# A two-layer codebook convolution: the copies of the extra numerators, the two range watches and an image's last step are rearranged

## The chip, the core and the metric

The kernel runs on one core of a Trainium2 chip. The metric is the device time of one execution in microseconds; three executions of the kernel before give a median of 4144.86 us (4143.25 to 4152.45). Engines are named as in the profile: PE multiplies matrices, PEld loads its weights, DVE is the vector engine, ACT the scalar engine, POOL is GpSimd, SP only issues transfers here. Each engine works through its own queue in order.

## What is computed

Input x has 16 images of 256 channels on 28 x 28 pixels. Each image is normalized in groups of 8 channels, goes through two layers that approximate a 3 x 3 convolution, through a squeeze-and-excitation gate, and is added to x. One layer replaces each channel's 9-pixel patch by a softmax mixture of 16 centroids, and looks the mixture up in a table:

```python
def amm_conv3x3(x, centroids, w_sub):
    patches = conv_general_dilated_patches(x, (3, 3), (1, 1), 'SAME')
    p = patches.reshape(B, C, 9, Ho * Wo).transpose(0, 3, 1, 2)
    d = sum(p * p)[..., None] - 2.0 * einsum('bncs,cks->bnck', p, centroids) + sum(centroids * centroids)
    attn = softmax(-d, axis=-1)
    lut = einsum('cks,cso->cko', centroids, w_sub)
    return einsum('bnck,cko->bno', attn, lut)

out = relu(bn1(amm_conv3x3(_gn(x), centroids1, wsub1)))
out = bn2(amm_conv3x3(out, centroids2, wsub2))
out = relu(se_layer(out) + _gn(x))
x = x + out
```

The last two lines are an image's last step: gate times layer output, plus the normalized image, relu, plus the image.

## The kernel before, in words

The 256 channels lie in 11 groups (`ORDER`: groups 9 and 10 first, then 0 to 8), the 784 pixels in two runs of 384 and 400 columns (`PXT`). One layer of one image is a stage of 2 x 11 = 22 **slots**, a slot being one group of one run. Stages follow in the order layer 0 of image 0, layer 0 of image 1, layer 1 of image 0, layer 0 of image 2, layer 1 of image 1 and so on.

The group of a slot s passes these steps, each on its engine:

- `patches`: POOL issues a transfer of the group pair's patches from DRAM, four slots ahead (nine in layer 1).
- Layer 1 only, five slots ahead: `a_logits` (PE), `a_turn` (DVE, two transpositions, L397), `a_max` (DVE, two reductions, L405), then once per pair `m_turn`, `m_out`, `m_in`, which bring the largest logit back into the patches. This is the extra pass for the maxima. Layer 0 has none; there two watches guard the range instead.
- `b_logits` (PE, L378), `b_exp` (ACT, two exponentials, L444): slot s, positions 5 and 6.
- `b_num` (PE, L454): numerators and sums, slot s + 1, position 3. It needs the exponentials.
- `b_turn` (DVE), slot s + 1, position 4: one transposition out of PSUM into a tile `t` (L466), the reciprocal `rc` of three columns of sums per block (L470), and in layer 0 the two watches, L473 on the sums in `t` and L474 on `rc`, which put their maxima into a column of `ext`.
- `c_scale`, slot s + 1, position 4: for groups 9 and 10 POOL writes scaled numerators into `qx` (L501); these are the extra numerators. For groups 0 to 8 POOL scales `t` in place (L487), and ACT copies five extra numerators per half from `qx` over the columns of sums in `t` (L490).
- `c_turn` (DVE, L511), slot s + 2, position 2, before the next group's L466: transposes `t` back. It needs POOL's scaling and ACT's copy.
- `c_look` (PE, L522): the lookups, 36 per run, five slots later, three or four of them in a slot; the last ones of a run are followed by `evacuate` on ACT (L535, L545).

The order on every engine's queue is written out by hand: a `Plan` collects jobs under (slot, position) and `emit` issues them sorted by this key, and within one key in the order in which they were put there. So in slot s + 1 ACT's queue holds the copy L490 of group s, then the exponentials of group s + 1 behind it. `prep` places four shifts (ACT, positions 4 and 6) and 15 patch writes (ACT's transfer queue, position 8) in a stage. PSUM pairs rotate in a ring of three: two take the logits of a group, one its numerators.

`norm` does an image's group statistics. `close` finishes an image after layer 1, in slots of the next stage (layer 0 of the image after the next): `se_hidden` and `se_gate` in two slots at position 9, then in two slots `finish(b, k)`, for one half of the channels each: L351 on ACT over 784 columns, L352 and L353 on DVE over 784, and then `store` (POOL, L356).

After the plan a test of `ext` on DVE and PE decides whether a slow, always guarded version of the whole computation runs; with these inputs it does not.

Of the kernel before, what the change touches and what calls it, by code (L numbers as in the profile page):

```python
# [9 lines left out]
AF = mybir.ActivationFunctionType  # L10
ALU = mybir.AluOpType
AX = mybir.AxisListType
# [5 lines left out]
HW = H * W  # L18
# [7 lines left out]
NBG = 9  # L26
# [4 lines left out]
S_LIM = 1e26  # L31
# [8 lines left out]
SUM = 27  # L40
# [23 lines left out]
def kernel(  # L64
# [28 lines left out]
    nc = tc.nc  # L93
    B, C, _ = x.shape
# [22 lines left out]
    def bank():  # L117
        return pair()[:, 0]
# [10 lines left out]
    xs = {}  # L129
# [70 lines left out]
    ext = const.tile([P, 2, NSTAT], F32, name="ext")  # L200
# [106 lines left out]
    ys = {}  # L307
# [34 lines left out]
        nc.vector.tensor_scalar_mul(nb, nb, -1.0)  # L342
        se[b] = gt, nb

    def finish(b, k):

        gt, nb = se[b]
        y, _ = ys[b]
        _, rstd = nrm[b]
        xt = xs[b]  # L350
        nc.scalar.activation(y[:, k], y[:, k], AF.Identity, bias=nb[:, k : k + 1], scale=gt[:, k : k + 1])  # L351
        nc.vector.scalar_tensor_tensor(y[:, k], xt[:, k], rstd[:, k : k + 1], y[:, k], op0=ALU.mult, op1=ALU.add)  # L352
        nc.vector.scalar_tensor_tensor(y[:, k], y[:, k], 0.0, xt[:, k], op0=ALU.max, op1=ALU.add)  # L353

    def store(b, ob):
        nc.gpsimd.dma_start(ob.rearrange("(b p) n -> p b n", p=P), ys.pop(b)[0])  # L356
# [29 lines left out]
    def blocks(u):  # L386
        return (u["px"][1] + 31) // 32
# [74 lines left out]
    def b_turn(u, gi):  # L462

        nb = blocks(u)
        t = npool.tile([P, 26, 32], F32, tag="nt", name="nt")
        nc.vector.transpose(  # L466
            t[:, : 2 * nb].rearrange("p (h b) r -> p h (b r)", h=2), u.pop(("nm", gi))[:, :, : 32 * nb]
        )
        rc = small.tile([P, 26, 3], F32, name="rc")
        nc.vector.reciprocal(rc[:, : 2 * nb], t[:, : 2 * nb, SUM : SUM + 3])  # L470
        if u["col"][gi] is not None:
            col = u["col"][gi]
            nc.vector.tensor_reduce(ext[:, 0, col : col + 1], t[:, : 2 * nb, SUM : SUM + 3], axis=AX.XY, op=ALU.max)  # L473
            nc.vector.tensor_reduce(ext[:, 1, col : col + 1], rc[:, : 2 * nb], axis=AX.XY, op=ALU.max)  # L474
        u["nt", gi] = t, rc

    qxs = {}

    def c_scale(u, gi):
        g, nb = u["groups"][gi], blocks(u)  # L480
        t, rc = u["nt", gi]
        key = u["key"]
        if g == NBG:
            qxs[key] = xqpool.tile([P, 13, EXTRA], F32, tag="qx", name="qx")
        if g < NBG:
            v = t[:, : 2 * nb, :SUM].rearrange("p b (j s) -> p b j s", s=9)
            nc.gpsimd.tensor_tensor(v, v, rc[:, : 2 * nb].unsqueeze(3).to_broadcast([P, 2 * nb, 3, 9]), ALU.mult)  # L487

            w = qxs[key][:, :nb, 10 * g : 10 * g + 5]
            nc.scalar.copy(  # L490
                t[:, : 2 * nb].rearrange("p (h b) r -> p h b r", h=2)[:, :, :, SUM:],
                bass.AP(w.tensor, w.offset, [list(w.ap[0]), [5, 2], list(w.ap[1]), list(w.ap[2])]),
            )
            if g == NBG - 1:
                qxs.pop(key)
        else:
            u.pop(("nt", gi))
            for h in range(2):
                e = 2 * (g - NBG) + h
                nj = 3 if e < 3 else 1  # L500
                nc.gpsimd.tensor_tensor(  # L501
                    qxs[key][:, :nb, 27 * e : 27 * e + 9 * nj].rearrange("p b (j s) -> p b j s", s=9),
                    t[:, h * nb : (h + 1) * nb, : 9 * nj].rearrange("p b (j s) -> p b j s", s=9),
                    rc[:, h * nb : (h + 1) * nb, :nj].unsqueeze(3).to_broadcast([P, nb, nj, 9]), ALU.mult,
                )

    def c_turn(u, gi):
        nb = blocks(u)
        t, _ = u.pop(("nt", gi))
        q = qpool.tile([P, 832], F32, tag="q", name="q")  # L510
        nc.vector.transpose(q[:, : 64 * nb], t[:, : 2 * nb].rearrange("p b r -> p (b r)"))  # L511
        u["q", gi] = q
# [44 lines left out]
    class Plan:  # L557
# [4 lines left out]
        def at(self, slot, pos, f, *a):  # L562
            self.jobs.setdefault((slot, pos), []).append((f, a))
# [6 lines left out]
        def stage(self, l, b, pat, s0, maxed, cols):  # L570
            at = self.at
            for pi, px in enumerate(PXT):
                n0 = s0 + pi * NG
                of = {}
                for ui, gs in enumerate(UNITS):
                    u = {
                        "l": l, "b": b, "pi": pi, "px": px, "pat": pat, "key": (l, b, pi),
                        "groups": gs, "n": self.units, "col": [cols.pop() if cols else None for _ in gs],
                    }
                    self.units += 1  # L580
                    n = n0 + 2 * ui
                    for gi, g in enumerate(gs):
                        s = n + gi
                        of[g] = u, gi
                        if maxed:
                            at(s - LB, 0, a_logits, u, gi)
                            at(s - LB, 1, a_turn, u, gi)
                            at(s - LB, 8, a_max, u, gi)
                        at(s, 5, b_logits, u, gi)
                        at(s, 6, b_exp, u, gi)  # L590
                        at(s + 1, 3, b_num, u, gi)
                        at(s + 1, 4, b_turn, u, gi)
                        at(s + 1, 4, c_scale, u, gi)
                        if g < NBG:
                            at(s + 2, 2, c_turn, u, gi)
                    at(n - LEAD - (LB if maxed else 0), 9, patches, u)
                    if maxed:
                        e = n + len(gs) - 1 - LB
                        at(e, 9, m_turn, u)
                        at(e, 9, m_out, u)  # L600
                        at(e + 1, 5, m_in, u)
                for k, (g, o, h) in enumerate(LOOKS):
                    s, r = divmod(k * NG, len(LOOKS))
                    early = maxed and 2 * r < len(LOOKS)
                    at(n0 + LC + s, 1 if early else 7, c_look, *of[g], o, h)
# [12 lines left out]
        def close(self, b, ob, te):  # L618
            self.at(te + 1, 9, se_hidden, b)
            self.at(te + 2, 9, se_gate, b)  # L620
            for k in range(NB):
                self.at(te + 3 + k, 9, finish, b, k)
            self.at(te + 5, 9, store, b, ob)

    stages = [(0, 0)]
    for b in range(B):
# [21 lines left out]
    for si, (l, b) in enumerate(stages):  # L648
        t = si * NS
# [14 lines left out]


    worst = small.tile([P, 2], F32, name="worst")
    nc.vector.tensor_reduce(worst, ext, axis=AX.X, op=ALU.max)
    good = small.tile([P, 2], F32, name="good")
    nc.vector.tensor_scalar(good, worst, S_LIM, None, op0=ALU.is_le)
    ps = bank()  # L670
    nc.tensor.matmul(ps[0:1, 0:2], lhsT=ones, rhs=good, start=True, stop=True)
    count = small.tile([1, 1], F32, name="count")
# [83 lines left out]
```

## Time and profile before

| what | value |
|---|---|
| median of three executions | 4144.86 us (4143.25 to 4152.45) |
| the profiled execution, its time | 4143.49 us |
| its span from first to last instruction | 4141.9 us |
| instructions | 81729 |
| busy: PE, DVE, ACT, POOL | 3777.2, 3244.5, 1424.4, 1283.7 us |
| mean granted clock of PE | 0.975 of full speed |
| chain that ended last | PE 44%, DVE 38%, issue 6%, ACT 5%, DMA 4% |
| DMA over the span | 148 GB/s |

Busy is the time in which an engine executes; a matmul's end is modelled. The chain is followed back from the last instruction, at each step to what released it. A timeline row reads: start in us, length in us, engine, line of the kernel, operation, output<-input, shapes, how many instructions are merged in it, and in brackets how long the engine had stood idle before it and what ended this. Windows give each engine's busy time in a stretch, then the mean granted clock of PE, the share of DMA engines' time and the rate.

### The profile page before, as it was taken

How to read it: one execution, taken by the hardware profiler on the slowest of the kernel's cores; microseconds unless marked ns; L12 is line 12 of the kernel's file. 1: busy time of each engine (PE TensorE's matmuls, PEld its weight loads, DVE VectorE, ACT ScalarE, POOL GpSimd, SP SyncE). 2: the span in 40 equal slices, each digit the busy share in tenths (PEclk: the TensorE clock that was granted, in tenths of full speed). 3: DMA queues.
4: the chain of work that ended last, by engine and by line, in shares of the span. 5: the costliest groups of instructions: out<-in, count | busy, mean ns of one | idle time of the engine just before them, and what ended most of it. 6: DMA issues, size and time to landing. Idle time of an engine off the chain costs nothing.

```text
span 4141.9 us, 81729 instructions
## 1 busy us (share of the span) xinstructions
PE 3777.2 (91%) x33042; PEld 1342.1 (32%) x33042; DVE 3244.5 (78%) x4644; ACT 1424.4 (34%) x2385; POOL 1283.7 (31%) x1314
## 2 busy tenths in 40 slices
PE   2989999999998999999999999999999999999897
PEld 0333333333333333333333333333333333333232
DVE  2669697795978969688795977969779696887897
ACT  1433433334343333433334333342433334333232
POOL 2332323323233232333323233232332323333222
PEclk7999999999999999999999999999999999999999
DMA  7454545445453455434555454454534554345431
GB/s 245 150 165 145 163 117 155 159 133 183 130 166 121 136 183 147 154 114 142 178 150 170 116 156 151 132 183 129 166 121 137 182 153 155 107 140 179 147 89 55
DMA packets 361805, 611.05 MB, mean 148 GB/s; under 512 B 205370, under 2 KB 217802, under 8 KB 361162
## 3 DMA queue, kind: packets, MB, share of 16 engines
q0 software_dynamic: 75520, 321.15, 24.4%
q10 hardware_dynamic: 80490, 236.05, 17.2%
q1 hardware_dynamic: 205408, 48.52, 5.7%
q8 instruction: 263, 4.31, 0.4%
q14 instruction: 124, 1.02, 0.1%
HBM read 338.50 MB, written 271.94 MB: 147 GB/s over the span
## 4 chain that ended last, share of the span: by engine, by line
PE 44%; DVE 38%; issue 6%; ACT 5%; DMA 4%; ACTq 2%; POOL 0%; DVEq 0%; SPq 0%; POOLq 0%
PE acc L522 20%; PE pair L378 12%; PE pair L454 11%; DVE z L397 9%; DVE nt L466 8%; DVE mx L405 8%; DVE q L511 4%; DVE rc L470 4%; ACT e L444 4%; ACTq L301 2%; DMA pat<-side 2%; DVE mt L414 1%; DMA pt<-dm 1%; DVE y L352 1%; ACT y L351 1%
## 5 line engine op out<-in xcount | busy, mean ns | idle before, releaser
L522 PE MATMUL acc<-q,ws 128*128 128x384 f32 (+1 forms) x4608 | 1787.3, 520 | 6.0 <-ACT im L535 6.0
L378 PE MATMUL pair<-pt,wd 31*64 31x400 f32 (+1 forms) x16896 | 1335.2, 521 | 186.0 <-ACT e L444 77.6
L487 POOL TENSOR_TENSOR nt<-nt,rc 128x648 f32<-128x648 f32 (+1 forms) x576 | 773.5, 1343 | 1874.4 <-DVE ext L473 957.2
L444 ACT ACTIVATE e<-pair 128x768 f32<-128x768 f32 (+1 forms) x1408 | 1084.3, 818 | 401.7 <-PE pair L378 390.9
L522 PEld LDWEIGHTS acc<-q,ws 128*128 128x128 f32 x4608 | 813.6, 192 | 975.4 <-issue 566.4
L490 ACT COPY nt<-qx 128x120 f32<-128x120 f32 (+1 forms) x576 | 183.8, 319 | 2216.0 <-DVE rc L470 1145.5
L466 DVE STREAM_TRANSPOSE nt<-pair 128x768 f32<-128x768 f32 (+1 forms) x704 | 701.2, 996 | 283.1 <-PE pair L454 279.5
L454 PE MATMUL pair<-e,cw 64*32 64x384 f32 (+1 forms) x11264 | 791.3, 507 | 131.7 <-ACT e L444 127.9
L511 DVE STREAM_TRANSPOSE q<-nt 128x768 f32<-128x768 f32 (+1 forms) x576 | 569.6, 989 | 331.1 <-POOL nt L487 319.8
L397 DVE STREAM_TRANSPOSE z<-pair 128x768 f32<-128x768 f32 (+1 forms) x704 | 668.8, 985 | 70.4 <-PE pair L378 67.0
L378 PEld LDWEIGHTS pair<-pt,wd 31*64 31x64 f32 x16896 | 335.0, 131 | 1102.3 <-DVE z L397 385.5
L405 DVE TENSOR_REDUCE mx<-z 128x48 f32<-128x768 f32 (+1 forms) x704 | 644.1, 957 | 0.0
L470 DVE RECIPROCAL rc<-nt 128x72 f32<-128x72 f32 (+1 forms) x704 | 438.5, 623 | 24.2
L365 POOL DMA_DIRECT2D pt<-pat x384 | 299.4, 780 | 472.5 <-PE pair L378 405.5
L454 PEld LDWEIGHTS pair<-e,cw 64*32 64x32 f32 x11264 | 161.6, 105 | 646.3 <-ACT e L444 461.2
L501 POOL TENSOR_TENSOR qx<-nt,rc 128x324 f32<-128x324 f32 (+3 forms) x256 | 166.2, 668 | 466.5 <-DVE rc L470 339.3
L352 DVE SCALAR_TENSOR_TENSOR y<-xt,gn_rstd,y 128x784 f32<-128x784 f32 x32 | 33.1, 1034 | 86.1 <-ACT y L351 86.1
L414 DVE STREAM_TRANSPOSE mt<-mx 128x256 f32<-128x256 f32 x192 | 81.2, 423 | 6.5
L474 DVE TENSOR_REDUCE ext<-rc 128x1 f32<-128x72 f32 (+1 forms) x352 | 81.4, 231 | 0.0
L289 ACT COPY side<-im 128x756 f32<-128x756 f32 x64 | 52.6, 823 | 35.3 <-DMA pat<-im 35.3
L473 DVE TENSOR_REDUCE ext<-nt 128x1 f32<-128x72 f32 (+1 forms) x352 | 60.7, 173 | 0.0
L291 ACT COPY side<-im 128x756 f32<-128x756 f32 x64 | 52.7, 825 | 7.2 <-DMA pat<-side 7.2
(63 smaller groups left out, 397.1 us busy)
## 6 DMA issues: line engine op xcount, KB each, us to landing
pt<-pat POOLq DMA_DIRECT2D x160, 800.0 KB, 5.4
pt<-pat POOLq DMA_DIRECT2D x160, 768.0 KB, 4.9
pat<-side ACTq DMA_DIRECT2D x128, 771.8 KB
pat<-im ACTq DMA_DIRECT2D x64, 771.8 KB
pat<-side ACTq DMA_DIRECT2D x64, 404.2 KB
xt<-in_x POOLq DMA_DIRECT2D x32, 784.0 KB, 7.4
pat<-side ACTq DMA_DIRECT2D x64, 367.5 KB
dm<-mt SPq DMA_DIRECT2D x320, 64.0 KB
```

Source lines behind the costliest of these rows:

```text
L365: nc.gpsimd.dma_start(pt[:, : 2 * len(gs), :n], view(u["pat"], 2 * gs[0] * P * HW + px, [[HW, P], [P * HW, 2 * len(gs)], [1, n]]),)
L378: nc.tensor.matmul(ps[i // 2][64 * h : 64 * h + 64, i % 2, :n], lhsT=wd[l][32 * i : 32 * i + rows, 2 * g + h, :], rhs=u["pt"][32 * i : 32 ...
L397: nc.vector.transpose(z[:, : 64 * nb].rearrange("p (i m) -> p i m", i=2), ps[:, :, : 32 * nb])
L405: nc.vector.tensor_reduce(u["mx"][:, a : a + 2].rearrange("p i (c b) -> p i b c", c=2)[:, :, :nb], z[:, : 64 * nb].rearrange("p (i b c k) ...
L444: nc.scalar.activation(e[:, :, :n], ps[:, :, :n], AF.Exp, scale=2.0)
L454: nc.tensor.matmul(ps[32 * i : 32 * i + 32, h, :n], lhsT=cw[l][64 * h : 64 * h + 64, g, i, :], rhs=es[i // 2][64 * h : 64 * h + 64, i % 2, ...
L466: nc.vector.transpose(t[:, : 2 * nb].rearrange("p (h b) r -> p h (b r)", h=2), u.pop(("nm", gi))[:, :, : 32 * nb])
L470: nc.vector.reciprocal(rc[:, : 2 * nb], t[:, : 2 * nb, SUM : SUM + 3])
L487: nc.gpsimd.tensor_tensor(v, v, rc[:, : 2 * nb].unsqueeze(3).to_broadcast([P, 2 * nb, 3, 9]), ALU.mult)
L490: nc.scalar.copy(t[:, : 2 * nb].rearrange("p (h b) r -> p h b r", h=2)[:, :, :, SUM:], bass.AP(w.tensor, w.offset, [list(w.ap[0]), [5, 2], ...
L511: nc.vector.transpose(q[:, : 64 * nb], t[:, : 2 * nb].rearrange("p b r -> p (b r)"))
L522: nc.tensor.matmul(accs[key][:, :n], lhsT=ws[l][:, 2 * g + h, o * P : (o + 1) * P], rhs=u["q", gi][:, 32 * nb * h : 32 * nb * h + n], star ...
```

## The change

Four things. The copy L490 leaves `c_scale` and becomes a function `c_fill` of its own, placed at position 7 of the same slot, behind the exponentials of the next group (position 6). Both watches reduce `rc`, one with maximum, one with minimum, so that `t` has one reader fewer before it is overwritten. `finish` works on half the columns, and is placed four times, in four slots; `store` follows two slots later. The closing test treats the two rows of `ext` one after the other.

```diff
--- before.py
+++ after.py
@@ -342,15 +342,15 @@
         nc.vector.tensor_scalar_mul(nb, nb, -1.0)
         se[b] = gt, nb
 
-    def finish(b, k):
+    def finish(b, k, i):
 
         gt, nb = se[b]
-        y, _ = ys[b]
+        v = slice(i * (HW // 2), (i + 1) * (HW // 2))
+        y, xt = ys[b][0][:, k, v], xs[b][:, k, v]
         _, rstd = nrm[b]
-        xt = xs[b]
-        nc.scalar.activation(y[:, k], y[:, k], AF.Identity, bias=nb[:, k : k + 1], scale=gt[:, k : k + 1])
-        nc.vector.scalar_tensor_tensor(y[:, k], xt[:, k], rstd[:, k : k + 1], y[:, k], op0=ALU.mult, op1=ALU.add)
-        nc.vector.scalar_tensor_tensor(y[:, k], y[:, k], 0.0, xt[:, k], op0=ALU.max, op1=ALU.add)
+        nc.scalar.activation(y, y, AF.Identity, bias=nb[:, k : k + 1], scale=gt[:, k : k + 1])
+        nc.vector.scalar_tensor_tensor(y, xt, rstd[:, k : k + 1], y, op0=ALU.mult, op1=ALU.add)
+        nc.vector.scalar_tensor_tensor(y, y, 0.0, xt, op0=ALU.max, op1=ALU.add)
 
     def store(b, ob):
         nc.gpsimd.dma_start(ob.rearrange("(b p) n -> p b n", p=P), ys.pop(b)[0])
@@ -470,8 +470,8 @@
         nc.vector.reciprocal(rc[:, : 2 * nb], t[:, : 2 * nb, SUM : SUM + 3])
         if u["col"][gi] is not None:
             col = u["col"][gi]
-            nc.vector.tensor_reduce(ext[:, 0, col : col + 1], t[:, : 2 * nb, SUM : SUM + 3], axis=AX.XY, op=ALU.max)
-            nc.vector.tensor_reduce(ext[:, 1, col : col + 1], rc[:, : 2 * nb], axis=AX.XY, op=ALU.max)
+            nc.vector.tensor_reduce(ext[:, 0, col : col + 1], rc[:, : 2 * nb], axis=AX.XY, op=ALU.max)
+            nc.vector.tensor_reduce(ext[:, 1, col : col + 1], rc[:, : 2 * nb], axis=AX.XY, op=ALU.min)
         u["nt", gi] = t, rc
 
     qxs = {}
@@ -485,14 +485,6 @@
         if g < NBG:
             v = t[:, : 2 * nb, :SUM].rearrange("p b (j s) -> p b j s", s=9)
             nc.gpsimd.tensor_tensor(v, v, rc[:, : 2 * nb].unsqueeze(3).to_broadcast([P, 2 * nb, 3, 9]), ALU.mult)
-
-            w = qxs[key][:, :nb, 10 * g : 10 * g + 5]
-            nc.scalar.copy(
-                t[:, : 2 * nb].rearrange("p (h b) r -> p h b r", h=2)[:, :, :, SUM:],
-                bass.AP(w.tensor, w.offset, [list(w.ap[0]), [5, 2], list(w.ap[1]), list(w.ap[2])]),
-            )
-            if g == NBG - 1:
-                qxs.pop(key)
         else:
             u.pop(("nt", gi))
             for h in range(2):
@@ -503,6 +495,17 @@
                     t[:, h * nb : (h + 1) * nb, : 9 * nj].rearrange("p b (j s) -> p b j s", s=9),
                     rc[:, h * nb : (h + 1) * nb, :nj].unsqueeze(3).to_broadcast([P, nb, nj, 9]), ALU.mult,
                 )
+
+    def c_fill(u, gi):
+
+        g, nb, key = u["groups"][gi], blocks(u), u["key"]
+        w = qxs[key][:, :nb, 10 * g : 10 * g + 5]
+        nc.scalar.copy(
+            u["nt", gi][0][:, : 2 * nb].rearrange("p (h b) r -> p h b r", h=2)[:, :, :, SUM:],
+            bass.AP(w.tensor, w.offset, [list(w.ap[0]), [5, 2], list(w.ap[1]), list(w.ap[2])]),
+        )
+        if g == NBG - 1:
+            qxs.pop(key)
 
     def c_turn(u, gi):
         nb = blocks(u)
@@ -592,6 +595,7 @@
                         at(s + 1, 4, b_turn, u, gi)
                         at(s + 1, 4, c_scale, u, gi)
                         if g < NBG:
+                            at(s + 1, 7, c_fill, u, gi)
                             at(s + 2, 2, c_turn, u, gi)
                     at(n - LEAD - (LB if maxed else 0), 9, patches, u)
                     if maxed:
@@ -619,8 +623,9 @@
             self.at(te + 1, 9, se_hidden, b)
             self.at(te + 2, 9, se_gate, b)
             for k in range(NB):
-                self.at(te + 3 + k, 9, finish, b, k)
-            self.at(te + 5, 9, store, b, ob)
+                for i in range(2):
+                    self.at(te + 3 + 2 * k + i, 9, finish, b, k, i)
+            self.at(te + 7, 9, store, b, ob)
 
     stages = [(0, 0)]
     for b in range(B):
@@ -664,9 +669,10 @@
 
 
     worst = small.tile([P, 2], F32, name="worst")
-    nc.vector.tensor_reduce(worst, ext, axis=AX.X, op=ALU.max)
     good = small.tile([P, 2], F32, name="good")
-    nc.vector.tensor_scalar(good, worst, S_LIM, None, op0=ALU.is_le)
+    for i, (op, test, lim) in enumerate(((ALU.max, ALU.is_le, S_LIM), (ALU.min, ALU.is_ge, 1.0 / S_LIM))):
+        nc.vector.tensor_reduce(worst[:, i : i + 1], ext[:, i], axis=AX.X, op=op)
+        nc.vector.tensor_scalar(good[:, i : i + 1], worst[:, i : i + 1], lim, None, op0=test)
     ps = bank()
     nc.tensor.matmul(ps[0:1, 0:2], lhsT=ones, rhs=good, start=True, stop=True)
     count = small.tile([1, 1], F32, name="count")
```

## Rows read from the trace of the kernel before

**Rows 1.** The page's first part: busy time, share of the span, instructions of each engine.
```profile
PE 3777.2 (91%) x33042; PEld 1342.1 (32%) x33042; DVE 3244.5 (78%) x4644; ACT 1424.4 (34%) x2385; POOL 1283.7 (31%) x1314
```

**Rows 2.** Windows of one image, cut at starts of L466: six slots, 2, 4, 1, 4, 4, 7, 16.
```profile
core 0: us, PE busy (x) PEld busy (x) DVE busy (x) ACT busy (x) POOL busy (x), PEclk, DMA share, GB/s
2179.89:2207.34 27.45, 27.45 (x240) 10.13 (x232) 16.32 (x20) 11.33 (x19) 10.54 (x9) 1.00 0.22 63
1958.19:1966.60 8.41, 8.41 (x86) 3.36 (x91) 3.70 (x9) 5.17 (x7) 3.25 (x5) 1.00 0.55 166
1966.60:1984.61 18.01, 16.78 (x166) 6.25 (x166) 11.31 (x21) 8.33 (x17) 7.29 (x7) 1.00 0.89 292
1984.61:1989.89 5.28, 5.28 (x59) 2.24 (x46) 3.21 (x9) 2.02 (x5) 2.03 (x2) 1.00 0.92 349
1989.89:2014.26 24.37, 20.17 (x146) 7.26 (x154) 14.87 (x26) 8.89 (x14) 7.34 (x7) 0.86 0.57 197
2014.26:2031.96 17.70, 17.48 (x162) 6.52 (x167) 9.93 (x19) 7.69 (x12) 8.36 (x10) 1.00 0.41 137
2031.96:2078.50 46.54, 44.84 (x398) 14.95 (x395) 43.45 (x65) 13.21 (x23) 13.47 (x13) 1.00 0.39 117
2078.50:2179.89 101.39, 93.94 (x860) 32.47 (x864) 98.76 (x128) 32.10 (x54) 27.32 (x29) 1.00 0.49 143
```

**Rows 3.** Waits of DVE from 1958 to 2207: us in total, times, longest.
```profile
DVE q L511 <- POOL nt L487: 19.6, 14, 1.6
DVE nt L466 <- PE pair L454: 13.5, 17, 2.6
DVE y L352 <- ACT y L351: 6.0, 2, 3.4
DVE z L397 <- PE pair L378: 3.5, 3, 2.6
```

**Rows 4.** Timeline of a light slot with a copy, 2022 to 2028.
```profile
2022.59 1.05 DVE L466 STREAM_TRANSPOSE nt<-pair 128x832 f32<-128x832 f32 x1 [1.83 <-PE pair L454]
2023.68 0.64 DVE L470 RECIPROCAL rc<-nt 128x78 f32<-128x78 f32 x1
...
2024.49 1.39 POOL L487 TENSOR_TENSOR nt<-nt,rc 128x702 f32<-128x702 f32 x1 [1.30 <-DVE ext L473]
2024.50 0.32 ACT L490 COPY nt<-qx 128x130 f32<-128x130 f32 x1 [3.32 <-DVE ext L473]
2024.72 1.56 ACT L444 ACTIVATE e<-pair 128x800 f32<-128x800 f32 x2
...
2025.60 1.61 PE L454 MATMUL pair<-e,cw 64*32 64x400 f32 x16
...
2027.28 1.05 DVE L466 STREAM_TRANSPOSE nt<-pair 128x832 f32<-128x832 f32 x1 [0.32 <-PE pair L454]
```

**Rows 5.** Timeline of two slots without a copy, 2014 to 2023.
```profile
2015.14 1.57 ACT L444 ACTIVATE e<-pair 128x800 f32<-128x800 f32 x2 [1.89 <-PE pair L378]
...
2017.75 0.90 PE L454 MATMUL pair<-e,cw 64*32 64x400 f32 x16
...
2021.58 0.91 PE L454 MATMUL pair<-e,cw 64*32 64x400 f32 x16
```

**Rows 6.** Timeline of the first of an image's two last steps, 1994 to 1997.
```profile
1994.04 1.04 ACT L351 ACTIVATE y<-y,se_nb,se_gt 128x784 f32<-128x784 f32 x1 [0.67 <-ACT e L444]
...
1995.11 1.03 DVE L352 SCALAR_TENSOR_TENSOR y<-xt,gn_rstd,y 128x784 f32<-128x784 f32 x1 [3.38 <-ACT y L351]
1996.18 0.97 DVE L353 SCALAR_TENSOR_TENSOR y<-y,xt 128x784 f32<-128x784 f32 x1
```

**Rows 7.** Groups of instructions, whole span: busy us, mean ns, idle before.
```profile
L252 DVE BATCH_NORM_STATS2 gn_st<-xt 128x6 f32<-128x392 f32 x64 | 32.1, 544 | 10.7 <-DMA xt<-in_x 10.7
```

**Rows 8.** Timeline of a heavy slot with watches, 2046 to 2049.
```profile
2046.52 0.64 DVE L470 RECIPROCAL rc<-nt 128x78 f32<-128x78 f32 x1
2047.07 0.18 DVE L473 TENSOR_REDUCE ext<-nt 128x1 f32<-128x78 f32 x1
...
2047.34 1.80 DVE L405 TENSOR_REDUCE mx<-z 128x48 f32<-128x768 f32 x2
```

## The prediction, made before the changed kernel ran

> **What bounds the kernel now.** I read the page first: PE and DVE are both busy most of the span, 91% and 78% [rows 1], so the question is which of them waits for which, and where. I then cut one image out of the trace, from 1958.19 to 2207.34 us, at the starts of the transposition L466, of which there is one per slot; 44 slots make an image, 14 whole images lie between 317 and 3840 us, and the pieces in the first two stages and the last one add about one more. The windows [rows 2] show two regimes. In 23 **heavy** slots (46.54 and 101.39 us, 6.4 us each), those with the extra pass for the maxima (L397, L405), DVE is busy 93% and 97%: DVE sets them. In the other 21, **light**, slots (27.45 + 8.41 + 18.01 + 5.28 + 24.37 + 17.70 = 101.2 us) DVE is busy 59% (59.3 us), and PE, the other candidate, is not full either: 16.78 of 18.01 in one stretch, 20.17 of 24.37 in the one with the image's last step. So a light slot is a loop of waits. DVE's waits in this image [rows 3] say with whom: 19.6 us for POOL's scaling, 13.5 us for PE's numerators (L454), 6.0 us for ACT in the last step (L351).
>
> The timeline of a light slot [rows 4] shows the loop: L466 at 2022.59, reciprocal 23.68, the copy L490 at 24.50, only then the exponentials at 24.72, numerators at 25.60 (their second half waits for the second exponential), next L466 at 27.28: 4.69 us, 0.32 of it DVE waiting for PE. The exponentials stand behind the copy in ACT's queue, and the copy needs this slot's reciprocal and watch. Where a slot has no copy [rows 5], the exponential starts at 2015.14, 0.88 us after its L466 at 2014.26 (a boundary of rows 2) instead of 2.13 us after, and the slot from numerators to numerators is PE's own 3.83 us (2017.75 to 2021.58, three lookups). The slot before it has four and takes 4.50 (the two together 8.33, from 2014.26 to 2022.59). 36 lookups in 11 slots are three of the longer kind and eight of the shorter, 44.1 us, 4.01 per slot. That is PE's floor.
>
> **The change, part by part.** *Copies moved* (576 of them, POOL's scale stays where it was). The copy passes both exponentials and, in a few slots, a shift, and it stands now ahead of the patch writes that ACT issues and of next slot's work. Its wait for the reciprocal holds nobody: the reciprocal ends 1.73 us after L466, the exponentials at 0.88 + 1.56 = 2.44 us. Who waits for it is L511: the copy ends 2.44 + 0.32 = 2.76 us after L466, POOL at 24.49 + 1.39, 3.29 us after. It stays covered by 0.5 us; where a shift or an evacuation stands before it, it is late by a few tenths in one or two slots per stage.
> What is late next is the loop on DVE and POOL, L466, reciprocal, scale, L511, L466. In rows 4 it takes 27.28 - 22.59 less the wait of 0.32 and about 0.07 that two independent DVE instructions overlap when nothing is between them (L473 begins 0.09 before the reciprocal ends [rows 8]): 4.30 us with 400 columns; the same loop with 384, scaled by 384/400, is an estimated 4.1. PE needs 4.01 on average, so light slots with copies go to 4.3 and 4.1, and PE runs ahead. It can be ahead by 3.83 - 0.91 - 1.05 less two handovers of 0.1 (2021.58 + 0.91 to 2022.59 is one), about 1.7 us, before numerators find their bank pair unread; in slots without copies DVE needs only 3.70 / 2 = 1.9 us [rows 2], and catches that up.
> By the stretches of rows 2, in their order: 6 slots, 27.45 to 25.8 (6 x 4.30): -1.65. 2 slots without copies, 8.41 to 7.2 (a lead of about 1.2 used up): -1.2. 4 slots at 384, 18.01 to 16.5 (4 x 4.1 and one late copy, 0.1): -1.5. The gate's slot, whose wait runs over PE and ACT, 5.28: 0. Of the 17.70, the two without copies 8.33 to 6.9 (a lead of 1.4 used up), the other two 9.37 to 9.0: -1.8.
>
> *The last step in four parts* (the 24.37 us, 4 slots). Now DVE stands 3.38 us at the first L352, since L351 begins only at 1994.04, after the exponentials [rows 6]. Half an L351 costs between 0.52 (proportional) and 1.04 (no saving); I take 0.65. Half an L352 and half an L353 cost together between 1.0 and 2.0; the nearest row at 392 elements, L252 at 544 ns [rows 7], says about 1.1, and I take 1.12. A slot then runs: copy done 2.7 us after L466, Identity 3.35, two vector steps 4.5, L511 and next L466 at 5.4. With PE ahead the exponentials are early and the copy is held by the reciprocal, 1.73 + 0.1 + 0.32 = 2.1: Identity 2.75, steps 3.9, L466 at 4.8. Patch writes issued by ACT in the first two of these slots stand before the Identity: 0.5 more in the first, 0.1 in the second. 5.9 + 4.9 + 4.75 + 4.75 = 20.3: -4.1. The store moves two slots later on POOL's queue and has a whole stage until its buffer is needed: 0. At the very end of the kernel the first half starts 0.4 us sooner and four more vector instructions cost as much: 0.
> [...]
>
> *Watches.* Both now read the reciprocal. In light slots they lie under POOL's 1.39 us: 0. In heavy slots DVE is full. L473 starts at 2047.07, before the reciprocal's end at 46.52 + 0.64 = 47.16, and L405 follows at 47.34 [rows 8]. A watch that needs the reciprocal cannot start before 47.16: between 0 (if the pair still ends by 47.34) and 0.2 us; I take 0.14. 7 heavy slots per image have watches: +1.0. POOL no longer waits for the first watch, but starts 0.17 us after the reciprocal either way: 0. Where light turns heavy DVE waits 2.6 us for PE (L397 [rows 3]), inside the 46.54; DVE comes there about 1.0 later relative to PE than now, so that wait shrinks: -1.0. The last reduction, once per execution, is split: 0.
>
> **Sum.** -1.65 - 1.2 - 1.5 - 1.8 - 4.1 + 1.0 - 1.0 = -10.25 us per image, times 15: -154 us. Profiled execution 4143.5 us (span 4141.9, 1.6 around it; 1.4 under the median, 4144.9): 4143.5 - 153.8 = **3990 us**. About 0.2% is what a measurement of this kernel can tell from no change.
>
> **Rivals.** (a) *Only the direct wait goes*: of DVE's 13.5 us of waiting for numerators the four slots without copies hold 8.41 + 8.33 - 4 x 1.9 = 9.1; the other 4.4 vanish, PE gains no lead, and the last step pays in four waits what it saves in length. -4.4 + 1.0 = -3.4, x15: 4092. For it: rows 3 name POOL with the larger wait, and that stays. Against: rows 5 show PE at its own pace as soon as there is no copy.
> (b) *PE's floor*: leads are kept and light slots run at 4.01: 21 x 4.01 + 1 for the gate's small matmuls = 85.2 in place of 101.2, x15: 3904. [...] Against: DVE's and POOL's loop of 4.30.
> (c) *Slower*: the copy takes POOL's place as what L511 waits for. If the exponentials still started as in rows 4, held by something other than the copy, they would end at 2.13 + 1.56 and the copy at 4.0, 0.7 us after POOL's 3.29; 17 light copy slots x 0.7 x 15 = 178, with the watches 15: 4337. It decides from the point where the copy ends over 0.5 us later than forecast. Against it stands only rows 5's 0.88.
> (d) *Nothing moves*: gains of the light slots come back as longer waits at the start of the heavy ones (2.6 us now), since DVE alone sets those: 4143. Against: 10 us do not fit into that wait.
>
> **Chances.** Forecast 0.60 (by itself 3950 to 4035, from the bounds of Identity, vector halves and watches), (a) 0.18, (b) 0.12, (c) 0.06, (d) 0.04. Range 3915 to 4092: it takes in most of (b) and (a). Faster 0.90, same 0.04, slower 0.06.
>
> **What would show it.** Exponentials about 0.9 us after L466 in light slots; DVE's wait for numerators near zero in copy slots, its wait for POOL kept at 1.2 to 1.6 us; light copy slots of 4.1 and 4.3 us; four waits of DVE for ACT per image of under 1.2 us each, and no stretch of lower clock there; heavy watched slots 0.1 us longer. Wrong: L511 released by ACT's copy, or the four waits each still above 2 us.

## The result, and the profile after

The changed kernel takes 3929.17 us (median of 4 runs, 3925.3 to 3933.48) against 4146.02 us before (4 runs): a ratio of 0.9475 with a 95% interval of 0.9459 to 0.9492. The profiled execution took 3933.48 us, its span is 3931.8 us, 210 us under that of before. The forecast was 3990 us. The direction held, and the time lies within the stated range of 3915 to 4092 us; it lies below the 3950 to 4035 us that the forecast gave for its own sum, so the gain was larger than forecast.

The page's first part and the engines of its chain, kernel after; they answer to [rows 1].

```profile
PE 3570.4 (91%) x33042; PEld 1295.3 (33%) x33042; DVE 3261.3 (83%) x4710; ACT 1507.9 (38%) x2417; POOL 1283.9 (33%) x1314
...
DVE 53%; PE 28%; issue 6%; DMA 5%; POOL 3%; ACT 2%; ACTq 2%; POOLq 0%; DVEq 0%; SPq 0%
```

PE shows 207 us of busy time less with the same 33042 matmuls. The mean length of one did not change (L454 507 ns before, 506 after), but matmuls overlap (16 of them in 0.91 us in the slot below), and a set of 16 that has to stop for its second exponential covers more time: 1.61 us in [rows 4]. Over the span L454 is busy 791.3 us before and 648.8 after, L378 1335.2 and 1252.2. DVE is busy about as long as before. In the chain DVE and PE have changed places: 53% and 28%, against 38% and 44%.

The windows of the same image after, cut at starts of L466 as [rows 2] are, in the same order (6 slots, 2, 4, 1, 4, 4, 7, 16). Columns as there. The six slots are here those ahead of the others, in [rows 2] those behind them; the mean of 14 images is 27.48 us before and 25.53 after.

```profile
1831.72:1857.22 25.50, 25.50 (x235) 10.04 (x234) 15.69 (x19) 12.73 (x21) 10.58 (x9) 1.00 0.24 68
1857.22:1863.82 6.60, 6.34 (x67) 2.43 (x73) 3.85 (x9) 3.89 (x6) 3.25 (x5) 1.00 0.71 210
1863.82:1879.82 16.00, 15.91 (x174) 5.95 (x166) 11.28 (x21) 8.65 (x17) 7.28 (x7) 1.00 0.91 284
1879.82:1884.84 5.02, 5.02 (x59) 2.29 (x44) 3.32 (x11) 2.35 (x6) 2.03 (x2) 1.00 0.95 369
1884.84:1907.04 22.20, 17.73 (x161) 7.38 (x160) 16.20 (x29) 11.22 (x18) 6.65 (x6) 1.00 0.65 216
1907.04:1921.73 14.69, 14.28 (x150) 5.29 (x149) 10.11 (x19) 6.49 (x11) 8.84 (x11) 1.00 0.61 217
1921.73:1967.89 46.16, 40.38 (x382) 13.65 (x380) 44.16 (x66) 14.19 (x22) 13.70 (x13) 1.00 0.41 119
1967.89:2068.13 100.24, 93.43 (x870) 32.28 (x867) 98.20 (x129) 34.75 (x55) 27.29 (x29) 1.00 0.50 144
```

The light slots took 101.2 us and take 90.0, the heavy ones 147.9 and 146.4. In this image the last step's stretch has no part below full clock any more (mean granted clock 0.86, with 0.50 from 2000 to 2006 us; now 1.00), and PE's longest stand in it is 2.41 us (L454 behind L466). That isn't so in general. Of the 14 whole images the stretch was below full clock in ten before (0.86 in five, 0.93 in five) and is in ten after (0.92 or 0.93), as in this one:

```profile
455.57:477.80 22.23, 19.11 (x160) 7.74 (x160) 16.21 (x30) 11.02 (x18) 6.64 (x6) 0.92 0.63 208
```

The mean granted clock over the whole span is 0.975 before and after.

DVE's waits in that image, kernel after, from 1825 to 2066 (us, times, longest); they answer to [rows 3].

```profile
DVE q L514 <- POOL nt L487: 15.2, 11, 1.6
DVE y L352 <- ACT y L351: 5.6, 4, 3.5
DVE nt L466 <- PE pair L454: 4.2, 2, 2.5
DVE z L397 <- PE pair L378: 2.1, 2, 1.4
...
DVE q L514 <- ACT nt L503: 1.3, 1, 1.3
```

(L514 is the second transposition, L511 before; the copy is L503, L490 before.) The wait for numerators fell from 13.5 us in 17 waits to 4.2 in 2, both in slots without copies. The wait for POOL stayed, 15.2 us after 19.6. The wait for the last step's activation is four waits in place of two and about as long in sum, 5.6 after 6.0; one of them is 3.5 us. L514 was released by the copy once.

A light slot with a copy after, 400 columns, timeline 1912 to 1918; it answers to [rows 4].

```profile
1912.85 0.93 PE L378 MATMUL pair<-pt,wd 31*64 31x400 f32 x16
1913.04 1.05 DVE L466 STREAM_TRANSPOSE nt<-pair 128x832 f32<-128x832 f32 x1 [1.71 <-PE pair L454]
...
1914.12 0.64 DVE L470 RECIPROCAL rc<-nt 128x78 f32<-128x78 f32 x1
1914.16 1.56 ACT L444 ACTIVATE e<-pair 128x800 f32<-128x800 f32 x2 [2.54 <-PE pair L378]
...
1914.94 1.39 POOL L487 TENSOR_TENSOR nt<-nt,rc 128x702 f32<-128x702 f32 x1 [1.22 <-DVE rc L470]
...
1915.61 0.33 ACT L503 COPY nt<-qx 128x130 f32<-128x130 f32 x1
1915.85 0.91 PE L454 MATMUL pair<-e,cw 64*32 64x400 f32 x16
1916.36 1.04 DVE L514 STREAM_TRANSPOSE q<-nt 128x832 f32<-128x832 f32 x1 [1.19 <-POOL nt L487]
...
1917.33 1.01 DVE L466 STREAM_TRANSPOSE nt<-pair 128x832 f32<-128x832 f32 x1
```

The exponentials start 1.12 us after L466, as soon as PE has the logits, and no longer behind the copy. This is the first slot with a copy after two without; in the light copy slots where PE is further ahead they start between 0.6 us after L466 and 1.2 us before it (medians by slot over 14 images), where before it was 2.0 to 2.1 us after. Numerators stand ready at 1916.76; L466 begins only at 1917.33, right behind L514, and L514 began when POOL was done. The slot is 4.29 us of DVE and POOL, and PE is ahead.

### The profile page after: what moved, and what is told of

It reads as the page before. It is cut to its first block, busy times and chain, and to the rows that moved or that the text cites. A ratio compares the mean times of both kernels' runs of the same rounds, so it can differ in the third digit from the quotient of the medians.

```text
span 3931.8 us, 81773 instructions
## 1 busy us (share of the span) xinstructions
PE 3570.4 (91%) x33042; PEld 1295.3 (33%) x33042; DVE 3261.3 (83%) x4710; ACT 1507.9 (38%) x2417; POOL 1283.9 (33%) x1314
## 4 chain that ended last, share of the span: by engine, by line
DVE 53%; PE 28%; issue 6%; DMA 5%; POOL 3%; ACT 2%; ACTq 2%; POOLq 0%; DVEq 0%; SPq 0%
PE acc L525 14%; DVE z L397 13%; DVE mx L405 11%; DVE nt L466 10%; DVE q L514 10%; PE pair L378 9%; DVE rc L470 5%; PE pair L454 5%; POOL nt L487 3%; ACTq L301 2%; DMA dm<-mt 1%; DMA pat<-side 1%; DVE y L352 1%; ACT y L351 1%; DVE y L353 1%
## 5 line engine op out<-in xcount | busy, mean ns | idle before, releaser
L444 ACT ACTIVATE e<-pair 128x768 f32<-128x768 f32 (+1 forms) x1408 | 1111.4, 822 | 1913.6 <-PE pair L378 1734.0
L378 PE MATMUL pair<-pt,wd 31*64 31x400 f32 (+1 forms) x16896 | 1252.2, 519 | 246.1 <-DVE z L397 182.3
L514 DVE STREAM_TRANSPOSE q<-nt 128x768 f32<-128x768 f32 (+1 forms) x576 | 569.0, 988 | 292.7 <-POOL nt L487 253.0
L466 DVE STREAM_TRANSPOSE nt<-pair 128x768 f32<-128x768 f32 (+1 forms) x704 | 688.8, 978 | 126.5 <-PE pair L454 123.6
L454 PE MATMUL pair<-e,cw 64*32 64x384 f32 (+1 forms) x11264 | 648.8, 506 | 76.0 <-DVE nt L466 61.6
L397 DVE STREAM_TRANSPOSE z<-pair 128x768 f32<-128x768 f32 (+1 forms) x704 | 665.5, 983 | 56.8 <-PE pair L378 55.6
L378 PEld LDWEIGHTS pair<-pt,wd 31*64 31x64 f32 x16896 | 310.8, 130 | 1114.9 <-DVE z L397 625.2
L405 DVE TENSOR_REDUCE mx<-z 128x48 f32<-128x768 f32 (+1 forms) x704 | 643.9, 957 | 0.0
L470 DVE RECIPROCAL rc<-nt 128x72 f32<-128x72 f32 (+1 forms) x704 | 438.2, 622 | 24.2
L503 ACT COPY nt<-qx 128x120 f32<-128x120 f32 (+1 forms) x576 | 183.8, 319 | 332.3 <-DVE rc L470 332.1
L454 PEld LDWEIGHTS pair<-e,cw 64*32 64x32 f32 x11264 | 134.3, 105 | 476.8 <-issue 267.8
L352 DVE SCALAR_TENSOR_TENSOR y<-xt,gn_rstd,y 128x392 f32<-128x392 f32 x64 | 47.9, 749 | 77.6 <-ACT y L351 77.6
L473 DVE TENSOR_REDUCE ext<-rc 128x1 f32<-128x72 f32 (+1 forms) x352 | 81.3, 231 | 12.1
L474 DVE TENSOR_REDUCE ext<-rc 128x1 f32<-128x72 f32 (+1 forms) x352 | 77.6, 220 | 0.0
L289 ACT COPY side<-im 128x756 f32<-128x756 f32 x64 | 52.6, 823 | 51.0 <-DMA pat<-im 35.9
L351 ACT ACTIVATE y<-y,se_nb,se_gt 128x392 f32<-128x392 f32 x64 | 45.3, 712 | 38.1 <-issue 34.3
```

Source lines behind the costliest of these rows:

```text
L378: nc.tensor.matmul(ps[i // 2][64 * h : 64 * h + 64, i % 2, :n], lhsT=wd[l][32 * i : 32 * i + rows, 2 * g + h, :], rhs=u["pt"][32 * i : 32 ...
L397: nc.vector.transpose(z[:, : 64 * nb].rearrange("p (i m) -> p i m", i=2), ps[:, :, : 32 * nb])
L405: nc.vector.tensor_reduce(u["mx"][:, a : a + 2].rearrange("p i (c b) -> p i b c", c=2)[:, :, :nb], z[:, : 64 * nb].rearrange("p (i b c k) ...
L444: nc.scalar.activation(e[:, :, :n], ps[:, :, :n], AF.Exp, scale=2.0)
L454: nc.tensor.matmul(ps[32 * i : 32 * i + 32, h, :n], lhsT=cw[l][64 * h : 64 * h + 64, g, i, :], rhs=es[i // 2][64 * h : 64 * h + 64, i % 2, ...
L466: nc.vector.transpose(t[:, : 2 * nb].rearrange("p (h b) r -> p h (b r)", h=2), u.pop(("nm", gi))[:, :, : 32 * nb])
```

## The experiments

Seven of the eight runs change one part; the last joins three. Each was timed beside runs of the kernel before, and its ratio is to those. The medians of these runs of the kernel before lie between 4139.14 and 4146.02 us, so a difference between two sets by their medians can be some 7 us off; where a run is set against the changed kernel, the difference by the ratios stands beside it, in us of 4140.

**Each part alone.** First the copies, on the kernel before:

```diff
-            nc.scalar.copy(t[...SUM:], ...)          # in c_scale, position 4
+    def c_fill(u, gi): nc.scalar.copy(u["nt", gi][0][...SUM:], ...)
+                            at(s + 1, 7, c_fill, u, gi)
```

> The kernel before with the copies behind the exponentials, and nothing else (watches and last step as before). Theory (the copy held the exponentials, and so PE; without it PE runs ahead of DVE): 3905 to 3930 us, light slots with copies 4.25 and 4.0 us, the last step's two slots about 8.7 and 6.1 us since the whole activation is still to be waited for. Rival (the four parts carry the gain, by their shorter waits and PE's clock): 4000 us or more.

Measured: 3924.62 us, ratio 0.9482 (0.9459 to 0.9504). The whole gain of the change is here. The rival is out. The light copy slots are 4.25 and 4.0 us, the last step's two slots 8.47 and 6.00 in the mean of 14 images, close to what was expected. The last step's stretch, undivided, takes 22.44 us in that mean, against 24.60 before and 22.10 in the changed kernel, so most of what that stretch gained comes from the copies as well.

The watches on the kernel before (the closing test changes with them):

```diff
-            nc.vector.tensor_reduce(ext[:, 0, ...], t[:, : 2 * nb, SUM : SUM + 3], axis=AX.XY, op=ALU.max)
-            nc.vector.tensor_reduce(ext[:, 1, ...], rc[:, : 2 * nb], axis=AX.XY, op=ALU.max)
+            nc.vector.tensor_reduce(ext[:, 0, ...], rc[:, : 2 * nb], axis=AX.XY, op=ALU.max)
+            nc.vector.tensor_reduce(ext[:, 1, ...], rc[:, : 2 * nb], axis=AX.XY, op=ALU.min)
```

> The kernel before with both watches on the reciprocal, and nothing else. Theory: 0.14 us more in each heavy slot with watches (5 to 7 of them per image, 15 images: 10 to 15 us), and in light slots of layer 0 the copy, which no longer waits for the first watch, some 0.08 us sooner (10 slots per image: 12 us less); 4140 to 4155 us. Rival (POOL and ACT gain by having one reader less to wait for): under 4120 us.

Measured: 4137.11 us, ratio 0.9991 (0.9977 to 1.0005): nothing that can be told from no change, 3 us under the expected range, and as the theory's two small terms of either sign give. In its trace the heavy watched slots are 0.14 us longer (6.27 to 6.41, 6.73 to 6.87) and light ones of layer 0 0.08 us shorter (4.48 to 4.40).

The last step in four parts on the kernel before (`finish` on half the columns, four slots, as in the change's diff):

```diff
-                self.at(te + 3 + k, 9, finish, b, k)
+                for i in range(2):
+                    self.at(te + 3 + 2 * k + i, 9, finish, b, k, i)
```

> The kernel before with the last step in four parts, and nothing else. Theory: with the copy still ahead of the exponentials each part waits behind both, a slot of 6.7 us four times in place of 8.1, 7.3, 4.4 and 4.6: 2 to 3 us more per image, 4175 to 4195 us. Rival (shorter pieces let DVE and PE go on earlier, and PE keeps its clock): 4110 us or less.

Measured: 4133.38 us, ratio 0.9981 (0.9967 to 0.9995). Neither expectation held: no loss of 40 us, and a gain of only 0.2%. The trace shows the third of the four waits, and the L466 that ends the slot without a copy behind the fourth part:

```profile
1990.22 0.31 ACT L490 COPY nt<-qx 128x120 f32<-128x120 f32 x1 [3.83 <-DVE ext L473]
...
1990.44 1.50 ACT L444 ACTIVATE e<-pair 128x768 f32<-128x768 f32 x2
...
1991.83 0.71 ACT L351 ACTIVATE y<-y,se_nb,se_gt 128x392 f32<-128x392 f32 x1
...
1992.57 0.63 DVE L352 SCALAR_TENSOR_TENSOR y<-xt,gn_rstd,y 128x392 f32<-128x392 f32 x1 [2.26 <-ACT y L351]
...
2003.64 1.05 DVE L466 STREAM_TRANSPOSE nt<-pair 128x832 f32<-128x832 f32 x1 [0.88 <-PE pair L454]
```

The mechanism was there: copy, exponentials, then L351, and four waits of 2.3 to 3.6 us, 10.4 us an image against 6.0. A part's slot took 6.14 us, not 6.7, and the next slot, without a copy, only 2.83 in place of 4.50, which I read as PE having got ahead while DVE stood. The five slots from the first part on sum to 7.48 + 6.14 + 6.14 + 6.20 + 2.83 = 28.8 us; undivided they were 8.08 + 7.29 + 4.43 + 4.57 + 4.50 = 28.9. In the mean of 14 images it is 28.1 and 29.1. My expectation had left out that payback.

**Two parts taken back.** The changed kernel with `finish` undivided:

```diff
-                for i in range(2):
-                    self.at(te + 3 + 2 * k + i, 9, finish, b, k, i)
+                self.at(te + 3 + k, 9, finish, b, k)
```

> The changed kernel with the last step undivided again, in two slots. Theory: the four parts are worth about 0.6 us per image, 3930 to 3945 us. Rival (the four parts carry much of the gain): 3970 us or more.

Measured: 3942.05 us, ratio 0.9521 (0.9498 to 0.9543). The four parts are worth about 13 us once the copies have moved (19 by the ratios). The gain isn't in the waits for L351: DVE stands 71.0 us in 29 of them here and 77.6 in 57 in the changed kernel. Its waits for POOL before L514 are 278.6 us in 201 here and 253.0 in 180 there, so the parts probably pay by lying in those waits; no run tests that. And with the watches as before (the second watch and the closing test go back too):

```diff
-            nc.vector.tensor_reduce(ext[:, 0, ...], rc[:, : 2 * nb], axis=AX.XY, op=ALU.max)
+            nc.vector.tensor_reduce(ext[:, 0, ...], t[:, : 2 * nb, SUM : SUM + 3], axis=AX.XY, op=ALU.max)
```

> The changed kernel with the watches as before, one on the sums and one on the reciprocal. Theory: heavy slots with watches 0.14 us shorter, light ones the same, 10 to 15 us less than the changed kernel: 3912 to 3922 us. Rival (freeing the tile of its second reader helps POOL start sooner): 3930 us or more.

Measured: 3911.22 us, ratio 0.945 (0.9433 to 0.9467), 18 us under the changed kernel by the medians, 10 by the ratios, whose intervals overlap. That the watches' new form costs time shows in a heavy slot of the changed kernel, DVE's timeline 1935 to 1937, to be laid beside [rows 8]:

```profile
1935.34 0.64 DVE L470 RECIPROCAL rc<-nt 128x78 f32<-128x78 f32 x1
1936.02 0.23 DVE L473 TENSOR_REDUCE ext<-rc 128x1 f32<-128x78 f32 x1
...
1936.17 0.22 DVE L474 TENSOR_REDUCE ext<-rc 128x1 f32<-128x78 f32 x1
1936.31 1.80 DVE L405 TENSOR_REDUCE mx<-z 128x48 f32<-128x768 f32 x2
```

L473 starts 0.04 us after the reciprocal's end, not 0.09 before it. From L470 to L405 it is 0.97 us, before 0.82. Five heavy slots per image are 0.14 us shorter without it (6.41 to 6.27, 6.87 to 6.73), 0.7 us per image and some 10 us in all.

The two traces lie further apart than that, 22 us, and 11.7 of them are in a slot without a watch, the one with the next image's group statistics (L259 on PE, L261 on DVE). Two of these slots in the changed kernel:

```profile
545.84:553.58 7.74, 7.40 (x60) 3.00 (x56) 5.90 (x11) 1.62 (x2) 1.08 (x2) 0.78 0.13 24
1262.18:1268.23 6.05, 5.71 (x60) 2.26 (x56) 5.80 (x12) 1.62 (x2) 1.08 (x2) 1.00 0.12 18
```

The granted clock parts them, 0.78 (0.50 from 548 to 550) and 1.00; what PE did just before does not, L378 having stood 1.86 and 1.87 us for L397 ahead of them. The long kind is there in ten of the 14 images of the kernel before (7.69 to 9.06 us, granted clock 0.64 to 0.78), in eight of the changed kernel (7.68 to 7.74 us, 0.78), and in one of this run (8.05 us). Whether the watches have to do with it isn't shown.

**What limits the light slots now.** The four parts two slots later, past the patch writes:

```diff
-                    self.at(te + 3 + 2 * k + i, 9, finish, b, k, i)
-            self.at(te + 7, 9, store, b, ob)
+                    self.at(te + 5 + 2 * k + i, 9, finish, b, k, i)
+            self.at(te + 9, 9, store, b, ob)
```

> The changed kernel with the four parts two slots later, past the last patch writes of the next layer, the last two parts in slots without copies. Theory (two patch writes on ACT's queue hold the first part by 3 us): no wait of DVE for the activation over 1.2 us, the slot of 7.5 us gone, some 2.6 us less per image: 3885 to 3900 us. Rival (the first part is late because of the gate or because PE's lead is used up): a long wait stays with the first part wherever it stands, 3915 us or more.

Measured: 3879.2 us, ratio 0.9374 (0.935 to 0.9397), some 50 us under the changed kernel (42 by the ratios), and 6 us under the expected range. What held the first part is seen in the changed kernel's timeline, 1886 to 1892:

```profile
1886.51 0.31 ACT L503 COPY nt<-qx 128x120 f32<-128x120 f32 x1 [0.39 <-DVE rc L470]
1886.53 3.02 ACTq L301 DMA_DIRECT2D pat<-side  x2
...
1889.60 0.71 ACT L351 ACTIVATE y<-y,se_nb,se_gt 128x392 f32<-128x392 f32 x1 [2.78 <-issue]
...
1890.34 0.63 DVE L352 SCALAR_TENSOR_TENSOR y<-xt,gn_rstd,y 128x392 f32<-128x392 f32 x1 [3.53 <-ACT y L351]
```

ACT stood idle for 2.78 us while its queue issued two patch writes, and DVE behind it for 3.53. In the run with later parts the waits for L351 in that image are these (view of DVE's waits, 1800 to 2040), and the slot of 7.54 us is 3.99:

```profile
DVE q L514 <- ACT nt L503: 2.3, 1, 2.3
DVE y L352 <- ACT y L351: 1.7, 2, 1.0
```

The first line is what remains: in this image two patch writes took 4.64 us to issue and the next one 1.12, and the copy behind them was late. The rival is out: in all 14 images that slot is 3.99 or 4.00 us, and the longest wait for a part in its new place is 1.0 us in that image. The granted clock of the same stretch is 1.00 in 13 of 14 images, where it was in four; how much of the gain is the clock's isn't separated.

Then the second transposition behind the first of the next group:

```diff
-                            at(s + 2, 2, c_turn, u, gi)
+                            at(s + 2, 4.5, c_turn, u, gi)
```

> The changed kernel with the second transposition (L514) behind the next group's first one, reciprocal and watches in DVE's queue. Theory (the loop of DVE and POOL sets a light slot, since L514 waits for POOL ahead of the next L466): that wait goes, light slots go to PE's 4.0 us, and L514 fills DVE's wait in the last step: 3 to 4 us less per image, 3870 to 3890 us. Rival (light slots are at PE's floor already, or the lookups then wait for L514): 3920 us or more.

Measured: 3880.41 us, ratio 0.9373 (0.9349 to 0.9397), 49 us under the changed kernel (42 by the ratios). DVE's waits in its image, 1791 to 2026, and its first three and last two light stretches by the same cuts:

```profile
DVE nt L466 <- PE pair L454: 21.1, 15, 2.6
DVE y L352 <- ACT y L351: 3.1, 1, 3.1
```

```profile
1798.65:1823.31 24.66, 24.66 (x240) 9.45 (x232) 15.52 (x20) 11.32 (x19) 10.40 (x9) 1.00 0.25 70
1823.31:1831.75 8.44, 8.44 (x86) 3.38 (x86) 4.85 (x9) 5.17 (x7) 3.43 (x6) 1.00 0.57 169
1831.75:1847.41 15.66, 15.57 (x166) 5.89 (x158) 10.45 (x19) 8.54 (x17) 7.30 (x7) 1.00 0.92 297
...
1851.87:1871.14 19.27, 17.67 (x174) 7.18 (x159) 15.71 (x30) 10.82 (x18) 6.66 (x6) 1.00 0.72 250
1871.14:1885.19 14.05, 14.05 (x144) 5.39 (x150) 9.97 (x20) 6.82 (x11) 8.24 (x10) 1.00 0.68 232
```

No wait for POOL is left; DVE waits for PE, and PE is busy without a break in most stretches. With the gate's slot, 4.46, the light slots take 86.5 us. So the loop of DVE and POOL did set them in the changed kernel, and PE's floor, 85.2 by the working of rival (b), is where they stop.

All three together (old watches, later parts, later transposition; only the first new line of the watches is shown):

```diff
+            nc.vector.tensor_reduce(ext[:, 0, ...], t[:, : 2 * nb, SUM : SUM + 3], axis=AX.XY, op=ALU.max)
+                    self.at(te + 5 + 2 * k + i, 9, finish, b, k, i)
+                            at(s + 2, 4.5, c_turn, u, gi)
```

> The changed kernel with all three: old watches, the last step two slots later, the second transposition behind the next first one. Theory: light slots at PE's floor of 4.0 us (21 slots in 85 us), heavy watched slots 0.14 us shorter: 3835 to 3860 us. Rival (the three gains are one and the same time): 3875 us or more.

Measured: 3849.39 us, ratio 0.93 (0.9281 to 0.932): the fastest of all, about 80 us under the changed kernel (72 by the ratios). Its light slots take 85.3 us in that image. The three gains (18, 50 and 49 us; 10, 42 and 42 by the ratios) do not add up. The later parts and the later transposition shorten the same eight slots, the last step's and the four behind them: 36.8 us in the mean of 14 images of the changed kernel, 34.3 with the first, 33.3 with the second and 32.3 with both, where eight slots at PE's 4.01 are 32.1.

## Why the prediction was right, and where it was off

**Copies.** Right in mechanism. The exponentials started 1.12 us after L466 in the slot shown (forecast 0.88, before 2.13) and mostly sooner, the copy ended ahead of POOL in all light slots of the image but two (by 0.00 and 0.11 us) and in all but 40 of the 576 of the kernel, and light copy slots went to 4.25 to 4.3 us at 400 columns. At 384 columns they went to 3.96 to 4.03 where the scaled loop had said 4.1. The run with the copies alone shows the cause.

**PE's lead.** Right, and undersized. By the stretches of the image, forecast and measured (us): 6 slots -1.65 and -1.96; 2 slots without copies -1.2 and -1.81; 4 slots -1.5 and -2.01; the last four -1.8 and -3.01. In the slots without copies I let 1.2 and 1.4 us of lead be used; the full lead of about 1.7 was there. The first of the two slots from 1857.22 is 2.07 us, which is DVE's own work. The gate's slot, which I put at 0, gave -0.26. The bound that I had worked out showed too: in the image PE waits 5 times, 5.1 us in all, for L466 to read its pair.

**The last step.** Forecast -4.1, measured 24.37 - 22.20 = -2.17: the step that failed. Three of the four slots are 4.88 us (14.66 for the three together), forecast 4.9, 4.75 and 4.75. The first is 7.54, forecast 5.9: "patch writes issued by ACT in the first two of these slots stand before the Identity: 0.5 more in the first" was too small by far; the two took 3.02 us to issue, and the run with later parts took this wait away. The 0.5 had no row behind it. So the sign of "four waits of DVE for ACT per image of under 1.2 us each" held for three and failed for the first, with 3.53 us, and "no stretch of lower clock there" failed in ten images of 14, with 0.92 or 0.93; what sets the granted clock no run shows. Half an L351 measured 0.71 us (I took 0.65), half an L352 and an L353 0.61 + 0.57 alone (1.12 taken). The last step's gain over one undivided step is small: 13 us. What I booked as the last step's gain was in the main the copies' again: with these alone, and the step undivided, the stretch gains 2.2 us in the mean, with all parts 2.5.

**Watches.** Forecast +1.0 per image; the slots show +0.14 in five of seven, 0.7 per image. The other term of this part, -1.0 from a shorter wait where light turns heavy, was right: the first heavy slot went from 7.24 to 6.15 us.

**Heavy slots.** I put the 16 of layer 1 at 0; they gained 1.15 us, from 101.39 to 100.24. Before, PE waited 4.1 us in 9 waits for exponentials, to get back a bank pair for the next logits; after, no such wait is in the view of PE's waits. Of the gain 0.78 us is in one slot, 6.83 us before and 6.05 after in every image: there L466 waited 0.42 us for numerators of a PE that had stood for an exponential behind the copy and a shift (kernel before):

```profile
2119.25 0.98 DVE L466 STREAM_TRANSPOSE nt<-pair 128x768 f32<-128x768 f32 x1 [0.42 <-PE pair L454]
```

I had seen the copy only as a brake of the light slots.

**The sum.** These stretches give -12.75 us for the image where I had -10.25; over the 14 whole images the mean is -13.6 (from 251.6 us an image to 238.0). That the light slots alone agree, -11.2 against -10.25, is in part luck: what PE's lead gave was undersized by 2.6 us, the last step oversized by 1.9. The profiled executions differ by 210 us where I had 154. 14 images with 3.4 us more each make 47 of the 56 us between; the first two stages, which I counted with the last as one image, gave 16 us by themselves (first L466 to the third stage's: 243.5 to 227.4, nearly all their slots being light) and the rest of the kernel 3, together 9 more than the 10 that I had for them. The last 4 of the 61 us between forecast and median are the profiled execution, the slowest of its four.

**Rivals.** (a) asked for no lead: refuted by the stretches without copies. (b), at 3904, is nearer to the measured time than the forecast, but not by its mechanism: the light slots take 90.0 us, where my sum has 91.0 and (b) 85.2; moving L514 reached it. (c) needed L514 released by the copy as a rule: 22 of its 576 executions waited for the copy, 39.7 us in all. (d) is out: the light slots' gain did not come back in the heavy ones.

**Half widths.** Half of L352's width costs 0.61 us against 1.03: two halves cost 0.19 us more than one whole, and the division gained all the same.

## What to carry to other kernels

Look along an engine's queue for a small instruction that waits early and stands before a large one that has nothing to do with it: 0.32 us of copy here held some 215 us of kernel. When such a wait goes, work out the next loop and how far the freed engine can run ahead before it must wait for a buffer, because stretches where the other engine has little to do pay that lead back (here 1.81 us in the first two slots without copies). An engine that issues transfers between its computations is not free for as long as the issuing takes (3.02 us here for ACT and two patch writes); place what others wait for away from them.

## What the runs showed of the hardware that was not expected

Issuing one patch write from ACT (L301, from `side`) took 0.25 us at the least and up to 4.13 us (median 0.35; in the kernel before up to 2.72). In the slot where two took 3.02 us, the activation behind them in the queue started 0.05 us after their end; the DMA engines were 92% busy in that slot (1884.84 to 1892.38).

In the changed kernel an L352 at half width (DVE, it reads `xt` and `y`) that began when a POOL scaling had 0.31 to 0.60 us still to run took longer than alone, and ended after that scaling. First L352 as a group (count, then ns least, median, most), then two of them beside POOL in the image above (timeline 1893.9 to 1900.4):

```profile
L352 DVE SCALAR_TENSOR_TENSOR y<-xt,gn_rstd,y x64: 614/734/1023, 461.1 to 3922.0; 128x392 f32<-128x392 f32 x64
```

```profile
1894.13 1.30 POOL L487 TENSOR_TENSOR nt<-nt,rc 128x648 f32<-128x648 f32 x1 [6.23 <-DVE rc L470]
...
1895.12 0.73 DVE L352 SCALAR_TENSOR_TENSOR y<-xt,gn_rstd,y 128x392 f32<-128x392 f32 x1 [0.76 <-ACT y L351]
...
1899.03 1.29 POOL L487 TENSOR_TENSOR nt<-nt,rc 128x648 f32<-128x648 f32 x1 [2.87 <-DVE rc L470]
...
1899.89 0.85 DVE L352 SCALAR_TENSOR_TENSOR y<-xt,gn_rstd,y 128x392 f32<-128x392 f32 x1 [0.65 <-ACT y L351]
```

Both end 0.42 us after POOL: 1895.85 after 1895.43, and 1900.74 after 1900.32. So do all 42 of the 64 that are longer than 0.65 us, within 0.41 to 0.44; alone an L352 takes 0.61 to 0.63. POOL's scale stays at 1.29 to 1.30 us beside them. POOL came first in those 42; no L352 or L353 here began before a scaling that it overlapped. The 42 are 8 us longer in all than they would be at 0.62 each.
